# A scan block with its additions moved to GpSimd, and its norm's scale and shift to ScalarE

## The chip, the cores and the metric

The kernel runs on one core of one Trainium2 chip. A core has TensorE (PE), VectorE (DVE), ScalarE (ACT), GpSimd (POOL) and a queue that issues transfers (SyncE, SP). The metric is the device time of one execution in microseconds (us); lower is better. The median of three executions of the kernel before is 11580.11 us (11578.98 to 11580.71).

## The reference

The input is x (8 images, 64 x 64 places, 96 channels). Layer 0 is a two-dimensional selective scan, layer 1 a linear attention and a feed-forward net with simulated 8-bit floats. Cut to what matters here:

```python
xz = group_norm(x) @ in_proj_w.T;  xh, z = split(xz)          # 192 channels each
xc = silu(depthwise_conv3x3(xh) + conv_b)
s0, s1 = xc[..., diag], xc[..., anti]                         # two orders of the 4096 places
xs = stack([s0, s1, reversed(s0), reversed(s1)])              # K = 4 directions
dts, Bs, Cs = split(einsum(xs, x_proj_weight))
delta = softplus(dt_projs(dts) + bias)
h = h * exp(delta * A) + (delta * u) * B                      # scan, 16 states a channel
y = einsum(h, C) + D * u                                      # summed over states, then directions
yn = (y - mean(y)) * rsqrt(var(y) + 1e-5) * ln_w + ln_b       # over the 192 channels
x = x + (yn * silu(z)) @ out_proj_w.T
t = x + attention(ln(x));  out = t + ffn_float8(ln(t))
```

## The kernel before, in words

**The scan loop.** `run` walks 128 steps: 8 images, two passes each (q = 0 forward, q = 1 backward over the time axis; both diagonal orders lie in the two halves of the 128 partitions), 8 chunks of 512 places a pass. A step has 16 iterations, one for each state n; an iteration handles three groups g of 128 partitions x 512 places. One iteration i does the following, spread over neighbouring iterations. ACT makes `decay` for i+2 (L985) and, for most states, `feedT` for i+2 (L1007: `duT` times the state's B; for n = 6 POOL does it, L998; for n = 0, 2, 4, 8, 10 DVE multiplies `du` by a row that PE spreads, L1017 and L1032). PE turns `feedT` into the PSUM banks `feed` (L1015). DVE scans (L1028). POOL keeps the last column as the next step's start value (`keep`, L1042) and multiplies the scanned states by C (`read`, L1047) for i-1. PE adds the turned product of i-4 into the PSUM tile `y` (`reduce`, L1061), of which there is one. `h` has six buffers, `decay` three, `cc` (the rows of C, fetched four iterations ahead, L976) five. Each engine runs its instructions in the order in which this loop writes them.

**The prologue of a step** (L905 on) is woven in as an urgent job: projections of the chunk, softplus on ACT with two loads of activation tables, then `du` (delta times u) on POOL (L947) in iteration 3 of the step before, its twelve turns on PE (L953) and three copies into `duT` on ACT (L955) in the iterations after it. `du` and `duT` have two buffers.

**The end of a step** (`place`, L1080 on) copies `y` to SBUF. After a forward step the copy goes to DRAM (`part`). In a backward step PE has added u times D (L1068), and the forward part, loaded at n = 0 into the same buffer tag `ys` and added by an identity matrix (L1074, three matmuls of 512 columns at n = 8, 9, 10); the result is written to DRAM in image order (`wide`).

**Side work.** `front` (convolution of the next image), `measures` (its group norm) and `tail` (`join`, attention and `layers` of the image before) are generators. `Work` places their pieces in the loop: each piece names its engine and an estimated length, `LAGS` says how many iterations it is put after the piece before it when the engine changes (ACT to DVE or POOL to DVE: one; an explicit lag of 0: the same iteration), and a credit for each engine limits how much is taken in an iteration. Two PSUM banks serve all side work. At the start of each image the loop finishes what is left of the side work (`finish`), and then starts the next image's.

**A join** (four tiles of 128 places, 8 joins an image) loads the two orders' outputs, adds them on PE with an identity matrix (L665), copies the sum to SBUF on ACT (L672) and takes its statistics from PSUM on DVE, in the same iteration (L675). POOL and ACT make the reciprocal root (`rsqrt`), ACT normalizes (L681), PE turns (L687), DVE multiplies by the gate silu(z) (L689), and PE projects. There the norm's scale ln_w is in the weights (`w_ln`, L701), and its shift enters as a second product of the gate with `b_ln` (L704). ACT copies the projection (L708), DVE takes statistics of the same PSUM bank in the same iteration (L713); `layers` does that too (L809, L813). The last image's tail runs after the loop, with more banks; there DVE adds the two orders (L656).

Of the kernel before, what the change touches and what calls it, by code (L numbers as in the profile page):

```python
# [17 lines left out]
P = 128  # L18
# [48 lines left out]
def weights(tc, const, dram, w):  # L67
# [29 lines left out]
    k.w_ln = tile("w_ln", [HC, 2, DM])  # L97
    k.b_ln = tile("b_ln", [HC, 2, DM])
# [93 lines left out]
    def layers():  # L192
# [8 lines left out]
        with tc.tile_pool(name="prep", bufs=1, side="right") as prep:  # L201
            w_out = load("w_out", [HC, 2, DM], w["w_out"], pool=prep)
            ln_w = load("ln_w", [HC, 2], w["ln_w"], pool=prep)
            ln_b = load("ln_b", [HC, 2], w["ln_b"], pool=prep)
            for _ in range(2):
                yield SPIN

            for a in range(2):
                nc.vector.tensor_scalar(k.w_ln[:, a, :], w_out[:, a, :], ln_w[:, a : a + 1], None, ALU.mult)
                nc.vector.tensor_scalar(k.b_ln[:, a, :], w_out[:, a, :], ln_b[:, a : a + 1], None, ALU.mult)  # L210
# [405 lines left out]
def tail(tc, work, x, out, k, at, b, last=False):  # L616
# [4 lines left out]
    with tc.tile_pool(name=f"t1_{b}", bufs=1, **area) as p1:  # L621
# [5 lines left out]
        with tc.tile_pool(name=f"t2_{b}", bufs=8 if last else 2, **area) as p2:  # L627
# [3 lines left out]
            def join(c):  # L631
# [22 lines left out]
                if last:  # L654
                    yield dve(2.5)
                    nc.vector.tensor_tensor(yn, ys[0], ys[1], ALU.add)  # L656
                    for i in range(4):
                        nc.vector.bn_stats(st[:, i, :], yn[:, i, :])
                        nc.vector.bn_aggr(mv[:, i, :], st[:, i, :])
                for j in range(0 if last else 2):  # L660
                    ps = yield bank(0.65)
                    v = view(ps, P, 2, DI)
                    for i in range(2):
                        for d in range(2):
                            nc.tensor.matmul(  # L665
                                v[:, i, :], k.ident, ys[d][:, 2 * j + i, :],
                                start=(d == 0), stop=(d == 1), skip_group_check=True,
                            )
                        if i == 0:
                            yield pe(0.65)  # L670
                    yield act(0.5)
                    nc.scalar.copy(yn[:, 2 * j : 2 * j + 2, :], v)  # L672
                    yield dve(1.0, 0)
                    for i in range(2):
                        nc.vector.bn_stats(st[:, 2 * j + i, :], v[:, i, :])  # L675
                        nc.vector.bn_aggr(mv[:, 2 * j + i, :], st[:, 2 * j + i, :])
                    work.release(ps)
# [5 lines left out]
                for a in range(2):  # L683
# [4 lines left out]
                    yield dve(0.7)  # L688
                    nc.vector.tensor_tensor(yg[:, a, :], v, gate[:, a, :], ALU.mult)  # L689
                    work.release(ps)  # L690
                ps = yield bank(0.65)
# [4 lines left out]
                for i in range(4):  # L696
                    if i % 2 == 0:
                        yield pe(1.2)
                    tok = slice(i * P, (i + 1) * P)
                    for a in range(2):  # L700
                        nc.tensor.matmul(  # L701
                            po[:, i, :], yg[:, a, tok], k.w_ln[:, a, :], start=False, stop=False, skip_group_check=True
                        )
                        nc.tensor.matmul(  # L704
                            po[:, i, :], gate[:, a, tok], k.b_ln[:, a, :], start=False, stop=(a == 1), skip_group_check=True
                        )
# [4 lines left out]
                yield dve(1.7, 0)  # L711
                for i in range(4):
                    nc.vector.bn_stats(st[:, i, :], po[:, i, :])  # L713
                    nc.vector.bn_aggr(mv[:, i, :], st[:, i, :])
                work.release(ps)
# [67 lines left out]
        with tc.tile_pool(name=f"t3_{b}", bufs=8 if last else 3, **area) as p2:  # L783

            def layers(c):
# [25 lines left out]
                yield dve(1.7, 0)  # L811
                for i in range(4):
                    nc.vector.bn_stats(st[:, i, :], po[:, i, :])  # L813
# [478 lines left out]
```

## Time and profile before

| what | value |
|---|---|
| median of 3 | 11580.11 us |
| the profiled execution | 11584.24 us |
| its span | 11582.5 us |
| mean granted TensorE clock | 0.913 |
| PE, DVE, ACT, POOL busy | 9540.5, 9483.5, 9430.0, 8885.1 us |
| L1028 scans on DVE | 6529.7 + 882.5 us |
| L1047 products on POOL | 7076.9 us, 3455 ns each |
| L985 + L1007 on ACT | 3971.1 + 3672.2 us |

The busy time of an engine is a union: two overlapping matmuls count once. The loop runs from 247 us to 11318 us of the span; in its middle an image takes some 1405 us. What comes before is the first image's convolution, what comes after the last image's tail.

### The profile page before, as it was taken

Reading aid. Unit: us, or ns where it says so; the run is one execution under the profiler, and the core shown is the slowest. Engines: PE = TensorE matmul, PEld = TensorE weight load, DVE = VectorE, ACT = ScalarE, POOL = GpSimd, SP = SyncE. Lnnn points to the kernel's source line nnn. Section 1 sums busy time; section 2 is a strip of 40 time slices with the busy share of each in tenths; the row PEclk is TensorE's granted clock in tenths of the full one; section 3 lists DMA queues with packets and bytes.
Section 4 is the critical chain, followed back from the end, with each engine's and each line's share of the span. In section 5 each row is a group of like instructions: output and inputs, shape, how many; then the busy total and the mean of one; then the engine's idle time right before and its main releaser. Section 6 shows DMA issues by size and latency. Waiting matters only on the chain.

```text
span 11582.5 us, 187413 instructions
## 1 busy us (share of the span) xinstructions
PE 9540.5 (82%) x63189; PEld 7973.6 (69%) x63189; DVE 9483.5 (82%) x10714; ACT 9430.0 (81%) x19571; POOL 8885.1 (77%) x6799
## 2 busy tenths in 40 slices
PE   6898889788888888888888888988889888887885
PEld 5677677676776667766677766767667676676663
DVE  2988888888878888788887888888888878888893
ACT  3888888878888888888888788887888878888883
POOL 1877887778867887777887788777887778878883
PEclk8999899898999989999899998999999889898996
DMA  3335333533335333353334433354333533332332
GB/s 91 105 91 140 100 91 91 144 107 97 98 96 134 108 105 91 106 135 104 97 98 113 125 100 104 92 133 116 100 92 98 131 107 96 100 97 86 99 97 53
DMA packets 1122757, 1207.26 MB, mean 104 GB/s; under 512 B 452789, under 2 KB 730006, under 8 KB 1121798
## 3 DMA queue, kind: packets, MB, share of 16 engines
q1 hardware_dynamic: 1121798, 1195.28, 37.6%
q8 instruction: 503, 8.24, 0.3%
q14 instruction: 456, 3.74, 0.1%
HBM read 874.83 MB, written 319.98 MB: 103 GB/s over the span
## 4 chain that ended last, share of the span: by engine, by line
PE 25%; POOL 21%; ACT 20%; DVE 15%; issue 11%; DMA 5%; SPq 3%; POOLq 0%; DVEq 0%; ACTq 0%
POOL h L1047 15%; DVE h L1028 9%; ACT feedT L1007 8%; PE y L1061 7%; PE feed L1015 6%; ACT decay L985 6%; DVE feed L1032 3%; DMA cc<-crow 3%; POOL du L947 2%; PE bank L550 2%; PE bank L915 2%; SPq L595 2%; POOL feedT L998 2%; PE bank L953 1%; POOL carry L1042 1%
## 5 line engine op out<-in xcount | busy, mean ns | idle before, releaser
L1047 POOL TENSOR_TENSOR h<-h,cc 128x1536 f32<-128x1536 f32 x2048 | 7076.9, 3455 | 368.8 <-DMA cc<-crow 187.1
L1028 DVE TENSOR_TENSOR_SCAN h<-decay,carry,feed 128x512 f32<-128x512 f32 x5376 | 6529.7, 1263 | 987.1 <-PE feed L1015 769.8
L985 ACT ACTIVATE decay<-delta,a_neg 128x512 f32<-128x512 f32 x6144 | 3971.1, 712 | 1156.1 <-DVE h L1028 1153.3
L1015 PE MATMUL feed<-ident,feedT 128*128 128x128 f32 x16896 | 3066.7, 301 | 1605.6 <-DVE h L1028 1070.5
L1061 PE MATMUL y<-ident,h 128*128 128x128 f32 x24576 | 3820.9, 288 | 127.2 <-POOL feedT L998 112.8
L1015 PEld LDWEIGHTS feed<-ident,feedT 128*128 128x128 f32 x16896 | 2178.8, 153 | 2288.1 <-ACT feedT L1007 882.8
L1007 ACT ACTIVATE feedT<-duT,rows 128x192 f32<-128x192 f32 x10240 | 3672.2, 444 | 23.8 <-PE feed L1015 21.2
L1061 PEld LDWEIGHTS y<-ident,h 128*128 128x128 f32 x24576 | 3127.9, 150 | 515.5 <-issue 335.2
L1042 POOL COPY carry<-h 128x3 f32<-128x3 f32 x2048 | 393.0, 192 | 1615.3 <-DVE h L1028 1545.8
L1032 DVE TENSOR_TENSOR feed<-feed,du 128x512 f32<-128x512 f32 x1920 | 1202.4, 687 | 137.2 <-PE feed L1017 134.6
L1028 DVE TENSOR_TENSOR_SCAN h<-decay,feed 128x512 f32<-128x512 f32 x768 | 882.5, 1201 | 127.3 <-PE feed L1015 87.5
L550 PE MATMUL bank<-wf,xp 97*128 97x192 f32 x4266 | 858.7, 332 | 0.0
L550 PEld LDWEIGHTS bank<-wf,xp 97*128 97x128 f32 x4266 | 691.0, 194 | 24.1 <-issue 13.5
L1017 PE MATMUL feed<-x,pick 77*128 77x512 f32 x1280 | 695.7, 626 | 3.4
L947 POOL TENSOR_TENSOR du<-delta,u 128x1536 f32<-128x1536 f32 x128 | 441.0, 3445 | 316.1 <-ACT delta L942 309.4
L915 PE MATMUL bank<-wx,u 128*128 128x77 f32 x3048 | 413.1, 299 | 36.2 <-DMA u<-seq 36.2
L915 PEld LDWEIGHTS bank<-wx,u 128*128 128x128 f32 x3048 | 407.3, 217 | 44.4 <-issue 39.6
L937 PE MATMUL bank<-x,ws 13*128 13x512 f32 x764 | 434.7, 649 | 1.6 <-ACT x L928 1.6
L998 POOL TENSOR_TENSOR feedT<-duT,rows 128x512 f32<-128x512 f32 x384 | 396.0, 1061 | 0.0
L955 ACT COPY duT<-bank 128x512 f32<-128x512 f32 x383 | 220.7, 576 | 176.4 <-PE bank L953 174.3
L939 DVE COPY delta<-bank 128x512 f32<-128x512 f32 x382 | 256.2, 671 | 56.4 <-PE bank L937 53.6
L1017 PEld LDWEIGHTS feed<-x,pick 77*128 77x128 f32 x1280 | 209.7, 197 | 71.7 <-DVE h L1028 39.5
(278 smaller groups left out, 7544.3 us busy)
## 6 DMA issues: line engine op xcount, KB each, us to landing
cc<-crow SPq DMA_DIRECT2D x4096, 128.0 KB
u<-seq SPq DMA_DIRECT2D x256, 384.0 KB
wide<-ys SPq DMA_DIRECT2D x512, 192.0 KB
ut<-image SPq DMA_DIRECT2D x768, 64.0 KB
seq<-us SPq DMA_DIRECT2D x128, 384.0 KB
part<-ys SPq DMA_DIRECT2D x64, 768.0 KB
y<-part SPq DMA_DIRECT2D x64, 768.0 KB
y<-wide SPq DMA_DIRECT2D x256, 192.0 KB
```

Of the source, the lines that this page charges most:

```text
L550: nc.tensor.matmul(v[:, j, :], flat[:, o : o + P], k.wf[:, i, :], start=(i == 0), stop=(i == 8), skip_group_check=True)
L915: nc.tensor.matmul(v[:, j, :], u[:, g, j * P : (j + 1) * P], w.wx[:, q, g, :], start=(g == 0), stop=(g == G - 1))
L947: nc.gpsimd.tensor_tensor(du, delta, u, ALU.mult)
L985: nc.scalar.activation(decays[i][:, g, :], made[m].delta[:, g, :], AF.Exp, scale=w.a_neg[:, q, g, n : n + 1])
L998: nc.gpsimd.tensor_tensor(f.rearrange("p (j g) (d c) -> p g j d c", g=G, d=d)[:, g], o.duT.rearrange("p (j g) (d c) -> p g j d c", g=G, d= ...
L1007: nc.scalar.activation(f[part], o.duT[part], AF.Copy, scale=o.rows[:, j, XB + d * NS + n : XB + d * NS + n + 1])
L1015: nc.tensor.transpose(feed[g][:, j * P : (j + 1) * P], feeds[i][:, j * G + g, :], w.ident)
L1017: nc.tensor.matmul(feed[0], w.pick[:, FEED[:n].count("D"), :], made[m].x, start=True, stop=True)
L1028: nc.vector.tensor_tensor_scan(h[:, g, back], a[:, g, back], feed[g][:, back], init, ALU.mult, ALU.add)
L1032: nc.vector.tensor_tensor(feed[g], feed[0], made[m].du[:, g, :], ALU.mult)
L1047: nc.gpsimd.tensor_tensor(hs[i], hs[i], c.unsqueeze(1).to_broadcast([P, G, T]), ALU.mult)
L1061: nc.tensor.matmul(y[:, j, :], hs[i][:, g, r * P : (r + 1) * P], w.ident, is_transpose=True, start=(n == 0 and j % 4 == 0), stop=(n == NS ...
```

## The change

1. The forward part is added to the backward pass's result by POOL, in SBUF, after `y` has been copied (a new urgent job `spread`, two additions of 128 x 768 a backward step); the three identity matmuls go. The part has its own buffer tag `y0` and is loaded at n = 8. In return `du` has one buffer, and its product waits until the step before has used `du` for the last time on DVE (`multiplied`).
2. In a join POOL adds the two orders (except in the last image, where DVE does, as before); PE's additions and ACT's copy go, and DVE takes the statistics from SBUF.
3. ln_w and ln_b are applied by ACT as scale and bias when it copies the turned rows out of PSUM, the gate is multiplied by POOL, and the projection has one product instead of two.
4. The statistics after the projection, and in `layers`, are taken from ACT's copy in SBUF, an iteration after it; the bank is released with the copy.
5. The side work of an image starts at iteration 7 instead of 5 of the image, after the last `spread`.

```diff
-        with tc.tile_pool(name="prep", bufs=1, side="right") as prep:
-            w_out = load("w_out", [HC, 2, DM], w["w_out"], pool=prep)
...
-            for a in range(2):
-                nc.vector.tensor_scalar(k.w_ln[:, a, :], w_out[:, a, :], ln_w[:, a : a + 1], None, ALU.mult)
-                nc.vector.tensor_scalar(k.b_ln[:, a, :], w_out[:, a, :], ln_b[:, a : a + 1], None, ALU.mult)
+        k.w_out = load("w_out", [HC, 2, DM], w["w_out"])
+        k.ln_w = load("ln_w", [HC, 2], w["ln_w"])
+        k.ln_b = load("ln_b", [HC, 2], w["ln_b"])
+        yield SPIN
...
-                for j in range(0 if last else 2):
-                    ps = yield bank(0.65)
...
-                    yield act(0.5)
-                    nc.scalar.copy(yn[:, 2 * j : 2 * j + 2, :], v)
-                    yield dve(1.0, 0)
...
+                else:
+                    yield gp(1.8)
+                    nc.gpsimd.tensor_tensor(yn, ys[0], ys[1], ALU.add)
+                    yield dve(2.1)
+                for i in range(4):
+                    nc.vector.bn_stats(st[:, i, :], yn[:, i, :])
+                    nc.vector.bn_aggr(mv[:, i, :], st[:, i, :])
...
-                    yield dve(0.7)
-                    nc.vector.tensor_tensor(yg[:, a, :], v, gate[:, a, :], ALU.mult)
+                    yield act(0.7)
+                    nc.scalar.activation(
+                        yg[:, a, :], v, AF.Identity, scale=k.ln_w[:, a : a + 1], bias=k.ln_b[:, a : a + 1]
+                    )
                     work.release(ps)
+                yield gp(2.3)
+                nc.gpsimd.tensor_tensor(yg, yg, gate, ALU.mult)
...
-                        nc.tensor.matmul(
-                            po[:, i, :], gate[:, a, tok], k.b_ln[:, a, :], start=False, stop=(a == 1), skip_group_check=True
+                            po[:, i, :], yg[:, a, tok], k.w_out[:, a, :], start=False, stop=(a == 1), skip_group_check=True
                         )
                 yield act(0.5)
                 nc.scalar.copy(t, po)
...
-                yield dve(1.7, 0)
+                work.release(ps)
+                yield dve(1.7)
                 for i in range(4):
-                    nc.vector.bn_stats(st[:, i, :], po[:, i, :])
+                    nc.vector.bn_stats(st[:, i, :], t[:, i, :])
...
         yield gp(3.4)
-        du = o.du = tile("du", [P, G, T])
+        while m and not made[m - 1].multiplied:
+            yield "G", 0.0, -1, False
+        du = o.du = tile("du", [P, G, T], 1)
...
+        if n == FEED.rindex("D"):
+            made[m].multiplied = True
...
-        if q and n in (8, 9, 10) and part == 2:
-            j = n - 8
-            nc.tensor.matmul(
-                y[:, 4 * j : 4 * j + 4, :].rearrange("p a c -> p (a c)"), w.ident,
-                other[m][:, j * T : (j + 1) * T], start=False, stop=False, skip_group_check=True,
-            )
...
-        if q == 0:
-            nc.scalar.copy(ys, y.rearrange("p j c -> p (j c)"))
-            nc.sync.dma_start(out=image(b).part[:, c, :], in_=ys)
-            return
...
+        if q == 0:
+            nc.sync.dma_start(out=image(b).part[:, c, :], in_=ys)
+        else:
+            work.start(spread(m, rows), urgent=True)
+
+    def spread(m, rows):
+        b, q, c = steps[m]
+        for d in range(2):
+            yield gp(1.8, 1)
+            nc.gpsimd.tensor_tensor(
+                rows[:, d], rows[:, d], other[m].rearrange("p (d k c) -> p d k c", d=2, k=TB)[:, d], ALU.add
+            )
...
-            if at == LAG + 1 and b:
+            if at == LAG + 3 and b:
+                work.finish(lambda: all_done() and not other)
                 work.finish(all_done)
                 work.stream(between(b))
```

## The prediction

> **What bounds the kernel now.** I read the page's parts 1, 4 and 5 first, then stretches of the span, then the waits, then the timeline of single steps.
>
> ```profile
> PE 9540.5 (82%) x63189; PEld 7973.6 (69%) x63189; DVE 9483.5 (82%) x10714; ACT 9430.0 (81%) x19571; POOL 8885.1 (77%) x6799
> PE 25%; POOL 21%; ACT 20%; DVE 15%; issue 11%; DMA 5%; SPq 3%; POOLq 0%; DVEq 0%; ACTq 0%
> ```
>
> Four engines are equally full and share the chain: no engine is the bound over the whole span, so time lies in what they wait for. The next view cuts out three stretches of the scan loop: the joins of one image, its layers, and four steps without side work (columns: from:to, length, busy of each engine, TensorE clock, DMA).
>
> ```profile
> 5044.40:5435.60 391.20, 322.46 (x2304) 273.46 (x2304) 320.55 (x420) 307.38 (x670) 303.45 (x303) 0.96 0.39 108
> 5483.20:5757.80 274.60, 222.26 (x1463) 180.82 (x1461) 239.73 (x270) 240.56 (x507) 237.32 (x207) 0.89 0.35 98
> 10883.40:11184.20 300.80, 245.87 (x1640) 201.11 (x1640) 274.22 (x265) 262.52 (x552) 257.19 (x144) 0.92 0.36 100
> ```
>
> Without side work DVE is busy 274.22 of 300.80 (0.912): DVE is the bound, a step (16 iterations) takes 75.2 us. In the joins it is busy 0.82 only; there something stops it. The waits name it:
>
> ```profile
> DVE h L1028 <- PE feed L1015: 857.3, 739, 10.9
> DVE st L713 <- ACT t L708: 135.8, 37, 11.8
> DVE st L675 <- ACT y L672: 109.5, 74, 5.2
> DVE st L813 <- ACT t L809: 71.7, 31, 12.1
> POOL carry L1042 <- DVE h L1028: 1545.8, 755, 13.7
> SPq L976 <- POOL h L1047: 1403.4, 470, 6.2
> ```
>
> Three are same-iteration waits: the statistics follow ACT's copy of the same bank, and that copy stands behind ACT's burst in iteration 3 of each step (softplus, two table loads, a feed, y's copies; 10.15 us). One of them in the timeline (start, length, engine, line):
>
> ```profile
> 5179.76 2.45 DVE L1028 TENSOR_TENSOR_SCAN h<-decay,carry,feed 128x512 f32<-128x512 f32 x2
> 5185.83 0.27 DVE L713 BATCH_NORM_STATS2 st<-bank 128x6 f32<-128x96 f32 x1 [3.61 <-ACT t L708]
> 5182.12 1.47 ACT L1094 COPY ys<-y 128x768 f32<-128x768 f32 x2
> 5183.49 1.95 ACT L985 ACTIVATE decay<-delta,a_neg 128x512 f32<-128x512 f32 x3
> 5185.34 0.46 ACT L708 COPY t<-bank 128x384 f32<-128x384 f32 x1
> ```
>
> POOL, on the other hand, waits 1545.8 us for scans: it has room on average. The rows that price the change:
>
> ```profile
> L947 POOL TENSOR_TENSOR du<-delta,u 128x1536 f32<-128x1536 f32 x128 | 441.0, 3445 | 316.1 <-ACT delta L942 309.4 <-DMA cc<-crow 5.4 <-DMA image<-pre 1.4
> L1074 PE MATMUL y<-y,ident 128*128 128x512 f32 x384 | 196.9, 595 | 0.0
> L704 PE MATMUL bank<-b_ln,gate 96*128 96x96 f32 x928 | 184.7, 282 | 0.0
> L665 PE MATMUL bank<-y,ident 128*128 128x192 f32 x896 | 182.4, 351 | 0.0
> L689 DVE TENSOR_TENSOR yg<-bank,gate 96x512 f32<-96x512 f32 x116 | 78.1, 674 | 17.5 <-PE bank L687 17.2
> L656 DVE TENSOR_TENSOR y<-y,y 128x768 f32<-128x768 f32 x8 | 7.7, 958 | 46.0 <-DMA y<-wide 46.0
> ```
>
> **The change, part by part.** The sum is made against the profiled execution, 11584.2 us (span 11582.5 and 1.7 around it), 4.1 above the median of 11580.1.
>
> POOL gains two-input operations at L947's 3445/1536 = 2.24 ns an element (no row has 768 or 1024 elements; the 384 of L854 take 914 ns, 2.38): 128 additions of 768 for the second pass's parts (1.73 us each, 221), 56 for the joins (97), 64 gates of 1024 (2.31, 148): 466 us, 8885 to 9351. DVE loses 128 gate products of 0.67 (86). PE loses the groups L665, L704 and L1074 (182 + 203 with the last image's + 197). ACT loses 112 copies of 0.47 (L672, 52), gains 128 evacuations at 0.58 to 0.68 (the 512-column copies and biased copies of L604 and L928; 0.63 taken, 81), and y's copy in the 64 first-pass steps becomes two of 0.78 for one of 1.42 (+0.15 each).
>
> *Joins* (seven images). The statistics now follow POOL's addition or ACT's copy an iteration later, so 245.3 us of DVE waits (L713, L675), 35 an image, can go. But POOL rises in the 391.2 us from 303.4 by eight times 1.73 + 2.31 and three steps' additions (3 x 3.46) to 346.1, above DVE's 310: it becomes the fullest. At the 0.912 that the bounding engine reaches without side work that is 379.5: 11.7 saved, 82 in seven images. Bounds: a share of 0.88 saves nothing; all 245 go at best. What PE and DVE lose counts nothing here, since POOL covers it; if POOL kept up, up to 86 of DVE would come on top.
>
> *Layers.* The same move of the statistics (L813, 71.7 us, 9 an image); POOL 237.3 + 10.4 = 247.7, over 0.912 = 271.6, 3 less than 274.6. Between 3 and 9: 6, times seven, 42.
>
> *du with one buffer.* It waits for the previous step's last DVE product, so in the order of the instructions it moves from iteration 3 to 10, its turns (0.6 us of PE each) from the ends of iterations 4 to 6 to those of 11 to 13, ACT's three copies (0.58) from 5 to 7 into 12 to 14. In the bare step, DVE idles 0.30 and 0.68 ahead of iterations 7 and 8 on turns queued behind these; they get 0.30 + 0.44 back. At 12 the copy stands ahead of the feed for iteration 14, where DVE already waits 1.80: 0.58 lost. Where L1074 leaves PE's end of iterations 12 to 14, iteration 0 gets its 0.44 too. Net -0.6 in a second-pass step, -0.16 in a first-pass one: about 15 of the former lie outside the stretches above, all 64 of the latter: -19. Bounds: -77 if all 128 steps gained the 0.6, +74 if the loss alone stays. What is queued behind du at its new place: POOL's later reads, PE's turns of feeds, so DVE.
>
> *y's copies.* The next sums wait for the bank and DVE for a turn behind them at iteration 5: +0.15 x 64 = +10.
>
> *At nothing:* SyncE's issues keep their number; the 4 stores of each half now stand behind POOL's addition, ahead of a fetch that is used four iterations (over 16 us) later and already waits for POOL (1403.4 us); the load of the first pass's part comes 8 iterations later, with 7 left. The convolutions' stretch keeps its work, moved by two iterations. The last image's tail: DVE 10.9 and PE 24 go, POOL 18.5 and ACT 10 come; it is a chain over all engines, 0, bounds -25 to +20.
>
> Sum: 11584 - 82 - 42 - 19 + 10 = 11451; less 4, **11447 us** on the median.
>
> One rule speaks against it. The Trainium skill (GPSIMD Engine Reference, 4.1 Engine selection) gives elementwise work to VectorE, GpSimd being about twice as slow with two inputs; the rows agree (958 against some 1730 ns for 768). Taken as a verdict, all 466 us would count against 317 of waits, 11733; POOL's waits for DVE speak against charging them in full.
>
> **Rivals.**
> *A, slower: du's turns wait for POOL.* Without side work POOL would end du 2.5 us before PE reaches its turn (11084.7 against 11087.2, from the timeline of that step with du's 3.45 put in). In the layers POOL is now 4.6 us behind DVE at that iteration (L1042 starts at 5490.6, the scan ended at 5486.0). With 12 to 14 us more in a join step it falls further behind, and each microsecond past 2.5 stops PE, the feeds and DVE. Some 49 steps are loaded; from 2.7 us in each (133/49) the gain is gone; at 5 it gives 11584 - 133 + 245 - 4 = 11692. Against it: a stall lets POOL catch up, and du no longer waits for softplus.
> *B, nothing gained.* ACT's burst itself holds the feeds, and DVE, freed of one wait, stands in `h <- feed` instead (857.3 us now): 11580. For it: that wait is the largest; against: the statistics' waits come on top of it in the timeline.
> *C, slower: TensorE's clock.* It is at half in places. The joins of images 5 and 6 do the same, with clocks of 0.94 and 0.90, in 288.8 and 293.8 us: 0.04 costs 1.7%. If PE with less work lost 0.04 in all of the loop's 11070 us: +190, 11637. Steps with and without L1074 show the same clock (0.92, 0.91), which speaks against it.
> The Trainium skill (TensorE: Matmul & The Clock Gate, Part 1) says that activity releases the throttle, and that is this rival's reason; the half clock after pauses agrees.
> *D, all waits go:* 11584 - 317 - 4 = 11263; it needs POOL at 0.97 in the joins, which no stretch shows (0.93 in the first step of an image).
>
> **How the numbers follow.** Forecast 0.47 (own range 11360 to 11540), A 0.27, B 0.10, C 0.06, D 0.10. 0.2% is about what the measurement can tell. Faster: 0.47 + 0.10 = 0.57; same: 0.07 of B; slower: A, C and the rest of B, 0.36. The range, 11310 to 11690, leaves out most of D and the upper half of A.
>
> **What would show it.** Right: the statistics' waits on ACT gone, POOL the fullest in the joins at over 0.9, these some 380 us, bare steps within a microsecond of 75. Wrong: PE waiting for du or its turns late in each step (A), the wait for feeds up by 300 (B), a clock under 0.89 (C), joins near 350 (D). DVE waiting for POOL's additions in the joins would be A's mechanism at another place.

## The result and the profile after

The changed kernel takes 11249.32 us (median of 4, 11245.66 to 11260.07), the kernel before 11579.55 beside it: a ratio of 0.972, with a 95% interval of 0.9703 to 0.9737. It is faster by 330 us, where 133 were forecast, and the time lies below the range. The profiled execution has a span of 11243.9 us at a mean clock of 0.907 (0.913 before), so a faster clock is no part of the gain.

The page's part 1 and the engines' line of its part 4, of the kernel after:

```profile
PE 9140.0 (81%) x60885; PEld 7661.4 (68%) x60885; DVE 9396.9 (84%) x10582; ACT 9455.9 (84%) x19651; POOL 9365.4 (83%) x7047
...
PE 24%; ACT 23%; DVE 17%; POOL 14%; issue 10%; DMA 7%; SPq 4%; DVEq 0%; POOLq 0%; ACTq 0%
```

POOL has grown by 480 us and PE has shrunk by 400. POOL's share of the chain nevertheless fell, from 21% to 14%. The stretches of the kernel after (from:to, length, busy of PE, PEld, DVE, ACT, POOL, then clock and DMA): the joins of image 3, its layers, and four steps without side work. They are the same iterations as the three rows of before in the prediction.

```profile
4914.50:5283.40 368.90, 298.24 (x2012) 252.67 (x2013) 313.39 (x417) 311.98 (x673) 344.52 (x336) 0.89 0.43 113
5320.20:5596.60 276.40, 220.13 (x1491) 182.12 (x1491) 249.90 (x291) 245.17 (x521) 251.99 (x219) 0.91 0.40 103
10564.10:10861.40 297.30, 242.75 (x1617) 203.05 (x1617) 273.29 (x265) 262.18 (x553) 270.93 (x153) 0.89 0.38 101
```

The joins went from 391.2 to 368.9 us, with POOL busy 344.5 (0.93), as the fullest. The layers did not gain (274.6 to 276.4). The bare steps went from 75.2 to 74.3 us each. The waits of the kernel after (engine, line, releaser: us in total, times, longest):

```profile
DVE h L1009 <- PE feed L996: 811.6, 729, 4.4
POOL carry L1025 <- DVE h L1009: 803.2, 438, 7.6
DVE st L654 <- POOL y L651: 110.2, 28, 6.5
PEld bank L934 <- POOL du L928: 73.8, 37, 3.9
PE bank L934 <- POOL du L928: 61.8, 35, 3.6
```

The three waits of statistics for ACT (135.8, 109.5 and 71.7 us) are gone from the loop; of the first and the third, 34.5 and 15.8 us are left, all in the last image's tail (24.9 and 12.1 before). One for POOL's additions, 110.2, is new. POOL's wait for scans has halved, from 1545.8 to 803.2. DVE's wait for feeds did not grow. PE's wait for `du`, rival A's mechanism, is there.

Where did the 330 us come from (338.6 between the two profiled executions)? An image's 256 iterations are cut by the starts of POOL's carry copies, and the differences to the kernel before are summed over the eight images (us, worked out from the two traces):

| iterations | what runs beside the loop | after minus before |
|---|---|---|
| 0-16 | border of two images | +23 |
| 16-85 | convolution | -32 |
| 85-125 | walk over the columns (`ut` loads) | -88 |
| 125-192 | joins | -150 |
| 192-200 | end of joins, attention | -71 |
| 200-256 | layers | -4 |
| after the loop | tail of the last image | -18.5 |

These cuts fall inside steps, and `du`'s 3.45 us on POOL stand on the other side of some of them after its move, so the split depends on them. Cut at whole steps (iterations 16, 80, 128, 192, 208 and 256) the same starts give -7, -143, -119, -62 and -13 in place of the five rows from -32 to -4. Either way the joins with their end give 181 to 221 us where 82 were forecast, and 88 to 143 come from a stretch that the prediction put at nothing.

### The profile page after: what moved, and what is told of

It reads as the page before. It is cut to its first block, busy times and chain, and to the rows that moved or that the text cites. A ratio compares the mean times of both kernels' runs of the same rounds, so it can differ in the third digit from the quotient of the medians.

```text
span 11243.9 us, 182845 instructions
## 1 busy us (share of the span) xinstructions
PE 9140.0 (81%) x60885; PEld 7661.4 (68%) x60885; DVE 9396.9 (84%) x10582; ACT 9455.9 (84%) x19651; POOL 9365.4 (83%) x7047
## 4 chain that ended last, share of the span: by engine, by line
PE 24%; ACT 23%; DVE 17%; POOL 14%; issue 10%; DMA 7%; SPq 4%; DVEq 0%; POOLq 0%; ACTq 0%
DVE h L1009 11%; ACT feedT L988 9%; POOL h L1030 8%; ACT decay L966 7%; PE y L1044 7%; PE feed L996 7%; DMA cc<-crow 4%; DVE feed L1013 4%; PE bank L542 3%; SPq L587 2%; PE bank L894 2%; PE feed L998 1%; ACT L63 1%; POOL du L928 1%; DMA y<-wide 1%
## 5 line engine op out<-in xcount | busy, mean ns | idle before, releaser
L996 PEld LDWEIGHTS feed<-ident,feedT 128*128 128x128 f32 x16896 | 2209.1, 155 | 2246.9 <-ACT feedT L988 840.8
L1044 PEld LDWEIGHTS y<-ident,h 128*128 128x128 f32 x24576 | 3164.5, 152 | 525.2 <-issue 410.3
L1025 POOL COPY carry<-h 128x3 f32<-128x3 f32 x2048 | 402.5, 197 | 877.0 <-DVE h L1009 803.2
L894 PE MATMUL bank<-wx,u 128*128 128x77 f32 x3048 | 360.0, 275 | 0.0
L894 PEld LDWEIGHTS bank<-wx,u 128*128 128x128 f32 x3048 | 352.3, 193 | 1.9 <-ACT duT L936 0.2
L934 PE MATMUL bank<-ident,du 128*128 128x128 f32 x1532 | 251.8, 291 | 65.1 <-POOL du L928 61.8
```

What stands on the lines that cost most here:

```text
L894: nc.tensor.matmul(v[:, j, :], u[:, g, j * P : (j + 1) * P], w.wx[:, q, g, :], start=(g == 0), stop=(g == G - 1))
L996: nc.tensor.transpose(feed[g][:, j * P : (j + 1) * P], feeds[i][:, j * G + g, :], w.ident)
L1044: nc.tensor.matmul(y[:, j, :], hs[i][:, g, r * P : (r + 1) * P], w.ident, is_transpose=True, start=(n == 0 and j % 4 == 0), stop=(n == NS ...
```

## The experiments

Ratios are to the kernel before, run beside each, with 95% intervals. "W" is the theory that the gain is DVE's same-iteration waits, "L" that it is the work taken off PE and DVE, "P" that it is the new place of `du`.

**The parts, each alone on the kernel before.** The part named in the change's list is applied, the rest is as before.

`only_stats`: part 4, here after the projection and likewise in the layers.

```diff
-                yield dve(1.7, 0)
+                work.release(ps)
+                yield dve(1.7)
                 for i in range(4):
-                    nc.vector.bn_stats(st[:, i, :], po[:, i, :])
+                    nc.vector.bn_stats(st[:, i, :], t[:, i, :])
...
-                work.release(ps)
```

> The kernel before, with the statistics after the projection and in the layers taken from ACT's copy in SBUF one iteration later, nothing else. Theory W (the gain is the same-iteration waits of DVE on ACT): the waits of L713 and L813 are 207 us, so 80 to 200 us faster. Theory L (the gain is work taken off PE and DVE): nothing is taken off, within 20 us of before. Theory P (the gain is du's new place, which frees the middle of each step): within 20 us of before.

Measured: 11599.44 us, 1.0025 (1.0016 to 1.0035), slower by 29. The waits at the two places did fall, from 207.5 us in sum to 43.4, but DVE's wait for the joins' copies rose from 109.5 to 187.5 and POOL's for `cc` from 187.1 to 295.0. The layers' first loads moved from iteration 194 to 197, and POOL now stops for them at iteration 201 (17.47 us in image 3). So removing waits can be undone by where the lag puts transfers.

`only_du`: `du` with one buffer, its product at iteration 10.

```diff
+        while m and not made[m - 1].multiplied:
+            yield "G", 0.0, -1, False
-        du = o.du = tile("du", [P, G, T])
+        du = o.du = tile("du", [P, G, T], 1)
```

> The kernel before, with du in one buffer and made in iteration 10, nothing else. Theory P: the stretch with the walk of an image (iterations 85 to 119) was 181.5 us before and 168.7 after the whole change, and no other part of the change touches it; image 0, which has no joins or layers, gained 32 us: some 100 us faster in all. Theory W and L: the forecast's -0.16 us in a first-pass step and at best no L1074 to remove in a second-pass one, so within 30 us of before.

Measured: 11561.17 us, 0.9992 (0.9983 to 1.0001). By stretches: -88 in iterations 85-125, -35 in the convolution, -58 in 192-200, but +47 in the joins and +103 in the layers. The -88 is the changed kernel's own: it comes with `du`'s place. In the kernel before, the time from DVE's last scan of iteration 87 to that of iteration 95 is 51.3 us on the mean of the eight images, in this one 38.2, in the changed one 37.4; the eight iterations that follow give 4 back. Most of the -71 of the changed kernel in 192-200 is here too.

`only_join`: part 2, POOL's addition of the two orders, with the statistics an iteration later.

```diff
-                for j in range(0 if last else 2):
-                    ...
-                    yield dve(1.0, 0)
+                else:
+                    yield gp(1.8)
+                    nc.gpsimd.tensor_tensor(yn, ys[0], ys[1], ALU.add)
+                    yield dve(2.1)
```

> The kernel before, with the two orders added by POOL in the joins and their statistics taken from SBUF, nothing else. Theory W: the 109.5 us of waits at L675 go and POOL gets 97 us in the joins, where it has room: 40 to 110 us faster. Theory L: 182 us of PE and 52 us of ACT go, of which little is on the path: 0 to 40 us faster. Theory P: nothing.

Measured: 11491.94 us, 0.9932 (0.9917 to 0.9947), -78.5.

`only_scale`: part 3, scale and shift on ACT, gate on POOL, one projection product.

```diff
-                    yield dve(0.7)
-                    nc.vector.tensor_tensor(yg[:, a, :], v, gate[:, a, :], ALU.mult)
+                    yield act(0.7)
+                    nc.scalar.activation(
+                        yg[:, a, :], v, AF.Identity, scale=k.ln_w[:, a : a + 1], bias=k.ln_b[:, a : a + 1]
+                    )
                     work.release(ps)
+                yield gp(2.3)
+                nc.gpsimd.tensor_tensor(yg, yg, gate, ALU.mult)
...
-                            po[:, i, :], gate[:, a, tok], k.b_ln[:, a, :], start=False, stop=(a == 1), skip_group_check=True
```

> The kernel before, with the norm's scale and shift applied by ACT and the gate by POOL, nothing else. Theory W: no same-iteration wait goes, so within 25 us of before. Theory L: 86 us of DVE and 203 us of PE go and POOL gets 148 us where it has room: 20 to 80 us faster; the last image's tail alone, 18.6 us shorter in the whole change, should show here.

Measured: 11517.17 us, 0.9953 (0.9936 to 0.9969), -53, of which -15.5 in the tail after the loop. That explains most of the changed kernel's -18.5 there.

`only_spread_du`: part 1 and part 5, POOL's addition of the forward part with `du`'s new place.

```diff
-        if q and n in (8, 9, 10) and part == 2:
-            ...
+            work.start(spread(m, rows), urgent=True)
```

> The kernel before, with the first pass's part added by POOL, and with du in one buffer as that needs the room: the whole change without the joins' and layers' parts. Less the run with du's move alone it gives the price of the additions. All theories: 197 us of PE go at a place where ACT sets the pace, 221 us of POOL come where it has room: within 30 us of the run with du's move alone. A POOL that is the bound would make it 50 to 200 us slower than that run.

Measured: 11515.08 us, 0.9958 (0.9941 to 0.9975), -52.5, or -43.5 beyond `du`'s place.

The parts alone sum to 29 - 78.5 - 53 - 52.5 = -155, less than half of 330. They need each other, and the other runs ask how.

**The same-iteration wait.** `lag_psum` is the kernel before with nothing but the lags: the same statistics from the same banks, one iteration after the copy.

```diff
-                yield dve(1.7, 0)
+                yield dve(1.7, 1)
...
-                    yield dve(1.0, 0)
+                    yield dve(1.0, 1)
```

> The kernel before, with all three kinds of statistics still read from PSUM, but one iteration after ACT's copy, the bank held until then. Theory W in its pure form, the wait alone and no work moved: 100 to 280 us of the 317 go. If the banks (two for all side work) bind, holding one longer gives part of it back, and it is less faster than the sum of the runs that take the statistics from SBUF. Theory L or P: within 20 us of before.

Measured: 11401.05 us, 0.9861 (0.9846 to 0.9875), -167. `after_same_iter` does the reverse: the changed kernel with part 4's statistics back in the copy's iteration.

```diff
-                yield dve(1.7)
+                yield dve(1.7, 0)
```

> The kernel after, with the statistics of the projection and of the layers put back into the iteration of ACT's copy (still read from SBUF): the same work on every engine. Theory W: DVE waits for ACT again as at L713 and L813, 207 us before: 80 to 200 us slower than after. Theory L or P: within 20 us of after.

Measured: 11410.84 us, 0.9865 (0.985 to 0.9879), some 168 us above the changed kernel by the ratios. Three numerals give half of the gain, and undoing two of them in the changed kernel costs as much again. So a lag of one iteration is worth about half. Not all of that is the wait, as W has it, for the lag also sets places: in `after_same_iter` the layers' first loads come at iteration 200 instead of 202, and POOL stops behind them at iteration 204, where the changed kernel has no stop:

```profile
5428.88 3.43 POOL L1030 TENSOR_TENSOR h<-h,cc 128x1536 f32<-128x1536 f32 x1 [11.56 <-DMA cc<-crow]
```

Against the changed kernel it loses 98 us in the steps of the joins (iterations 128 to 192) and 71 in the step with that stop (192 to 208). By the two profiles `lag_psum` gains 310 us in the iterations 16 to 256 and gives 117 back in the first 16, at the images' borders.

**POOL as the bound.** `after_gate_twice` lets POOL multiply by the gate twice (its output has an extra factor, so it only serves to price the work).

```diff
+                nc.gpsimd.tensor_tensor(gate, yg, gate, ALU.mult)
                 nc.gpsimd.tensor_tensor(yg, yg, gate, ALU.mult)
```

> The kernel after, with the gate's product in each join done twice by POOL (the output has an extra factor of the normalized rows and the gate): 64 x 2.31 = 148 us more of POOL, 130 of it in the joins under the loop. The forecast's step, POOL is the bound of the joins: 100 to 150 us slower than after. If POOL at 0.93 of the joins still has room and something else sets their time: under 40 us slower.

Measured: 11361.4 us, 0.9824 (0.981 to 0.9839), some 120 us above the changed kernel by the ratios. The joins of image 3:

```profile
4939.50:5324.90 385.40, 303.71 (x2011) 256.85 (x2012) 314.05 (x417) 311.68 (x672) 362.77 (x344) 0.87 0.38 108
```

18.2 us more of POOL made the stretch 16.5 longer. Adding work to POOL costs it nearly in full. Does taking work away pay as well? `after_gate_dve` gives the gate product to DVE, `after_join_dve` the joins' addition.

```diff
-                yield gp(2.3)
-                nc.gpsimd.tensor_tensor(yg, yg, gate, ALU.mult)
+                yield dve(1.1)
+                nc.vector.tensor_tensor(yg, yg, gate, ALU.mult)
```

> The changed kernel with the gate product by DVE (in SBUF) instead of POOL. POOL loses 64 of 2.37 us (152, 133 of it under the loop), DVE gets 64 of some 1.28 (958 ns for 768 elements), 82. POOL is at 0.93 in the joins, DVE at 0.85. If POOL alone bounds the joins: 344.5 - 19 = 325.5 over 0.93 is 350 a join for 368.9, -19 each, about -130 against the changed kernel. If DVE, now with 324 as full as POOL, sets the pace at 0.912: 355, -14 each, -95. If the two already hold each other up so that POOL's room buys nothing: +0 to +84 (10 more of DVE at 0.85).

Measured: 11201.72 us, 0.9688 (0.9673 to 0.9702). This version beats both kernels: 37 us below the changed one by the ratios, less than a third of the 130 that POOL as the only bound would give. Its joins:

```profile
4900.40:5263.10 362.70, 289.68 (x2011) 243.36 (x2012) 327.27 (x425) 311.50 (x672) 332.50 (x328) 0.92 0.41 115
```

```diff
-                    yield gp(1.8)
-                    nc.gpsimd.tensor_tensor(yn, ys[0], ys[1], ALU.add)
+                    yield dve(1.0)
+                    nc.vector.tensor_tensor(yn, ys[0], ys[1], ALU.add)
```

> The changed kernel with the joins' addition by DVE instead of POOL: POOL loses 56 of 1.74 us (97), DVE gets 56 of 0.96 (54). If POOL bounds the joins: -14 us of POOL each over 0.93, -15 a join, about -100 against the changed kernel. If DVE is next at 321 of 355: nearer -90; if DVE and POOL hold each other up: 0 to +60.

Measured: 11284.62 us, 0.9759 (0.9742 to 0.9775), some 45 above the changed kernel. DVE's 56 additions took 110.7 us instead of the 54 expected; the last section tells why.

**What the parts need of each other.** `lag_psum_du` joins the two that touch only order: lags of 1 and `du`'s new place (the edits of `lag_psum` and `only_du`).

```diff
-                yield dve(1.7, 0)
+                yield dve(1.7, 1)
...
+        while m and not made[m - 1].multiplied:
+            yield "G", 0.0, -1, False
```

> The kernel before with two edits: all statistics one iteration after ACT's copy, and du's new place. Alone the first gave -167 us and the second -9. If du's gain in the walk over the columns (-88 over eight images) is real and was only lost again behind the same-iteration waits in the joins and layers (+47 and +103), it stays here: -167 - 88 = -255, some 11313, ratio 0.978. If du's place has a cost of its own in loaded steps (rival A), the two only add: -176, some 11392, 0.985 or above.

Measured: 11472.24 us, 0.9918 (0.9904 to 0.9933), -93: `du`'s place makes this kernel 73 us slower than `lag_psum`. By stretches it gains 369 us in iterations 16 to 256 and loses 254 in the first 16. At the border the loop halts for layers that are not done: iteration 5 of image 3 takes 47 us from last scan to last scan (6.5 before). The joins end later in the planned order with the lag (last Gram sum at iteration 199, before at 183), and later again with `du`'s turns at their new place (211). The layers follow, and 159 of their instructions lie past iteration 256 in `lag_psum`, 286 here, none before. `lag_psum_du_border` moves the border two iterations on, as part 5 does.

```diff
-            if at == LAG + 1 and b:
+            if at == LAG + 3 and b:
```

> The kernel with lagged statistics and du's new place (-93), its images' border (where the planned order halts the loop until the last image's layers are done) moved from iteration 5 to iteration 7, as in the changed kernel. Theory F (the gain of lag and du is given back at the border: there 46.7 us stand in one iteration of each image, +254 us in the first 16 iterations over all images, for layers that reach four iterations past the border): most of it comes back, -93 - 200 or more, under 11280, ratio 0.975 or less. Rival A (du's new place costs in loaded steps): the border's stall only moves, -93, some 11472.

Measured: 11467.92 us, 0.9917 (0.9902 to 0.9931), no gain: the same 286 instructions are left, and iteration 7 takes 36 us in place of iteration 5. That time is given back at the border is seen in the trace; that two more iterations would cure it, as theory F had it, was wrong.

`join_stats` (the edits of `only_join` and `only_stats`) and `join_stats_du` (with `only_du`'s too) are the changed kernel without its scale part and without POOL's addition of the forward part, the first without `du`'s move.

```diff
+                    nc.gpsimd.tensor_tensor(yn, ys[0], ys[1], ALU.add)
...
+                    nc.vector.bn_stats(st[:, i, :], t[:, i, :])
```

> The kernel before with the joins' addition on POOL and all statistics one iteration later from SBUF, du at its old place. The two alone gave -78.5 and +29: -50 if they add, ratio 0.996. If it is the lag alone that counts, -167 as with the banks, 0.986. Against the same with du's new place (-133) it also gives what du's place is worth where nothing waits in the copy's iteration: -83 in the first case, +34 in the second.

Measured: 11408.19 us, 0.9858 (0.9842 to 0.9875), -157.

```diff
+        while m and not made[m - 1].multiplied:
```

> The changed kernel without the scale and gate part and without POOL's addition of the first pass's part: the joins' addition on POOL, all statistics an iteration later from SBUF, du's new place. Alone the two parts left out gave -53 and (with du) -52.5, or -43.5 beyond du. If these two add to the rest as they did alone, this stands at -330 + 53 + 43.5 = -234, some 11335, ratio 0.980. If the gain is nearly all from lag and du, it stands at -255 or more, 0.978 or less; if PE's and DVE's saved work is needed for most of it, at -165, the sum of the single parts, 0.986 or above.

Measured: 11432.15 us, 0.9884 (0.9869 to 0.9898), -133. Here too `du`'s move costs, 24 us, in spite of its gain in the walk. So `du`'s move earns nothing when it is alone (-9) or joined to the lag or to `join_stats`. What it is worth inside the whole change stays open, for no run has the changed kernel with `du` at its old place: the second buffer was given up for `y0`.

`after_no_spread` adds the scale part to that (the edits of `only_scale`; PE adds the forward part as before), `after_no_scale` POOL's addition of the forward part.

```diff
-            work.start(spread(m, rows), urgent=True)
+        if q and n in (8, 9, 10) and part == 2:
+            ...
```

> The changed kernel with the first pass's part added by PE into the bank as before (undoes POOL's addition of the parts, 221 us of POOL, and brings PE's 197 back), border at iteration 5. If the parts' gains add as they did alone: -330 + 43.5 = -287, ratio 0.975. If POOL is the bound, taking 221 us from it makes it faster than the changed kernel, under 0.972. If PE's work is what the rest needs gone, -186 (the kernel without both, -133, and the scale's -53), 0.984.

Measured: 11224.35 us, 0.9705 (0.969 to 0.9719), not to be told from the changed kernel. POOL's 221 us against PE's 197 is an even trade.

```diff
-                    yield act(0.7)
-                    nc.scalar.activation(
-                        yg[:, a, :], v, AF.Identity, scale=k.ln_w[:, a : a + 1], bias=k.ln_b[:, a : a + 1]
-                    )
+                    yield dve(0.7)
+                    nc.vector.tensor_tensor(yg[:, a, :], v, gate[:, a, :], ALU.mult)
...
+                            po[:, i, :], gate[:, a, tok], k.b_ln[:, a, :], start=False, stop=(a == 1), skip_group_check=True
```

> The changed kernel with the norm's scale and shift in the projection's weights and DVE's gate product as before. If the parts add as alone: -330 + 53 = -277, ratio 0.976. If this part with its fewer planned microseconds of PE and DVE (2 of 1.2 down to 0.65, 2 of DVE's 0.7 gone) is what lets the lagged chain keep its time: -133 - 43.5 = -176, ratio 0.985.

Measured: 11427.77 us, 0.9882 (0.9868 to 0.9897), -138. Taking the scale part away costs some 187 us by the ratios, though alone it gave 53. Two things are in it: places in the order, and work. In this kernel the layers' first loads are issued at iterations 197 to 201, and POOL stops for 17.4 us in iteration 201. SyncE's queue and POOL in the timeline (start, length, engine, line):

```profile
5398.48 7.43 SPq L783 DMA_DIRECT2D t<-mid  x1
5405.96 0.67 SPq L781 DMA_DIRECT2D xaT<-turned  x1
5406.67 8.34 SPq L783 DMA_DIRECT2D t<-mid  x1
5415.11 4.69 SPq L1096 DMA_DIRECT2D wide<-ys  x4
5419.84 6.86 SPq L964 DMA_DIRECT2D cc<-crow  x6
```

```profile
5427.63 3.46 POOL L1037 TENSOR_TENSOR h<-h,cc 128x1536 f32<-128x1536 f32 x1 [17.42 <-DMA cc<-crow]
5431.04 3.42 POOL L935 TENSOR_TENSOR du<-delta,u 128x1536 f32<-128x1536 f32 x1
```

The fetch of `cc` stands in SyncE's queue behind two loads of 7.43 and 8.34 us and four stores; POOL waits for it, and `du`, now right behind, reaches PE late (5.27 us of waiting in the trace): rival A's path, set off by a transfer. In the kernel before, the loads come at 194, in the changed one at 202. `no_scale_late2` keeps this kernel's work and puts the joins' end and the layers where the changed kernel has them, by two iterations more between gate and projection.

```diff
-                ps = yield bank(0.65)
+                ps = yield bank(0.65, 2)
```

> The changed kernel without the scale part (which alone of the four parts, taken away, costs nearly all: -138 for -330), but with two iterations more between the gate's product and the projection, which puts the joins' end at iteration 197 and the layers' first steps at 208, 212 and 216, where the changed kernel has them (191, 203, 204 and 220 without). The operations stay those of the kernel without the scale part. Theory O (the part counts by where it puts the joins and the layers' first loads in the planned order): most of it comes back, -280 to -330, ratio 0.976 or less. Theory L (by the 182 us of PE and 86 of DVE that it takes away): only the 20 us stall at iteration 201 goes, seven times some 10 to 15, so -138 - 100 at most, 0.980 or above.

Measured: 11373.08 us, 0.9828 (0.9813 to 0.9843), -198. So some 60 of the 187 us are places in the order (the layers' +53 are gone, and so is the stop), and some 125 are left for work. Which work? Its joins:

```profile
4945.70:5329.10 383.40, 313.91 (x2129) 269.83 (x2129) 320.51 (x431) 299.03 (x652) 326.45 (x328) 0.88 0.38 109
```

`after_gate_dve` has the joins and the layers at the same places. There DVE (327.3 for 320.5), POOL (332.5 for 326.5) and ACT (311.5 for 299.0) are busier; PE alone has less, 24.2 us (289.7), and the stretch is 20.7 shorter. By elimination what counts is PE's work, the second projection product. The granted clock differs too, 0.88 here and 0.92 there: by rival C's two rows (0.04 of clock for 1.7%) some 6.5 of the 20.7 us could be the clock's, an estimate, and these two runs do not separate them.

`gate_dve_no_spread` undoes both POOL additions that had bought little: the edits of `after_gate_dve` and `after_no_spread`.

```diff
-                nc.gpsimd.tensor_tensor(yg, yg, gate, ALU.mult)
+                nc.vector.tensor_tensor(yg, yg, gate, ALU.mult)
...
+        if q and n in (8, 9, 10) and part == 2:
```

> The changed kernel with the two POOL parts that bought nothing undone: the first pass's part is added by PE as before, the gate product is made by DVE in SBUF. Alone, against the changed kernel, -12 for the one and -41 for the other (ratios 0.9705 and 0.9688 to the kernel before, 0.972 for the changed one). If POOL's room counts: -50 together, ratio 0.967 to 0.968. If DVE, then the fullest, takes the place of POOL as the bound: no better than the one alone, 0.969 or above.

Measured: 11253.98 us, 0.9723 (0.9707 to 0.974): worse than `after_gate_dve` by some 40. With POOL relieved, PE's 197 us are no longer an even trade.

## Why the prediction was wrong

**Two steps failed.** Of the 197 us between forecast and result, the first step has to do with the joins, the second with a stretch that was put at nothing.

**The first: "What PE and DVE lose counts nothing here, since POOL covers it".** It made the fullest engine's busy time over 0.912 the length of a join stretch. Put into that sum, the measured share does give the length: 344.5 over 0.934 is 368.9, and 0.912 would have given 378. But the share is no constant of the bounding engine. POOL has 0.94 of the stretch in `after_gate_twice`, 0.92 in `after_gate_dve` and only 0.85 in `no_scale_late2`, which has PE's second product. In the joins POOL's work counts nearly in full (+18.2 gave +16.5), and PE's counts too (-24 gave -20.7, less what the clock may have), at a share of PE of only 0.82. That fits four engines that wait for each other in turn in every iteration; it was not followed instruction by instruction. The scale part's work, PE's second product above all (184.7 us by its row), was worth some 125 once the waits of the statistics were gone. Alone, with its places, the part gave 53. The sum's -82 measured -150 (-119 at whole steps), with the end of the joins -221 (-181).

**The second: "The convolutions' stretch keeps its work, moved by two iterations", at nothing.** In the walk over the columns it gave -88 (-143 at whole steps), the largest item that was not priced. In the kernel before, PE stands there once in each of six images for transfers, with the turns of the feeds queued behind it: for the `ut` that it turns, and for the `u` of the next step's projections. The same instructions of the changed kernel wait for nothing. Image 3 in the timeline, first before, then after (start, length, engine, line):

```profile
4864.00 1.09 PE L602 MATMUL bank<-ident,ut 128*128 128x128 f32 x4 [6.19 <-DMA ut<-image]
4878.96 4.90 PE L915 MATMUL bank<-wx,u 128*128 128x77 f32 x24 [3.93 <-DMA u<-seq]
```

```profile
4747.53 0.60 PE L594 MATMUL bank<-ident,ut 128*128 128x128 f32 x4
4751.79 2.89 PE L894 MATMUL bank<-wx,u 128*128 128x77 f32 x24
```

Summed over the images these waits are 73 us before and none after. They come and go with `du`'s place: every run with `du` at its old place has 64 to 75 us of them in iterations 80 to 128, every run with the new place none. DVE's wait for feeds in iterations 85 to 125 of image 3 shrank with them:

```profile
DVE h L1028 <- PE feed L1015: 30.7, 20, 8.2
```

```profile
DVE h L1009 <- PE feed L996: 16.3, 14, 2.2
```

POOL's own stop there did not go: it waits 16.47 us for `cc` behind the loads of `ut` before, and 16.02 after, one iteration later (the profile puts this one down to PE, but its scans had long been done, and `cc` is issued only behind a long run of `ut` loads). Why the new place of `du` puts PE's two groups behind their loads was not tested.

**The statistics' waits.** That they can go was right; with the places that the lag moves they are half of the gain, seen in both directions (-167 and +168). Of the 317 us, 37 lay in the last image's tail and stayed. The prediction let them go only as far as POOL's busy time allowed. Rival D priced all of them, and its 11263 is near the time, but its condition did not come (POOL at 0.93, not 0.97): its number is near by luck.

**Layers, -42: wrong.** The stretch took 1.8 us more. The statistics' wait went, but the layers' first loads moved from iteration 194 to 202, and some 30 of their instructions lie past iteration 256, in the next image's first iterations (+23).

**`du`'s move, -19.** The bare steps did as told, -0.87 us for a forecast -0.6. Not priced, besides the walk, was what the move costs elsewhere. Rival A's wait is there (PE 61.8 us, PEld 73.8 over mostly the same time), and the move cost 73 and 24 us in the two pairs of runs, but most of that stands at other places. In the first pair it is the border (254 us given back, 117 without the move), though PE waits only 54.2 us for `du`. In the second, the steps of the joins lose 129 us to the move and PE waits 24.6.

**The tail, 0 with bounds of -25 to +20:** -18.5, inside the bounds, nearly all from the scale part. **At nothing, SyncE's queue:** in the changed kernel that held, but only by where the loads fall. In `only_stats`, `join_stats_du` and `after_no_scale` they begin at iteration 197, five earlier than in the changed kernel, and from carry copy to carry copy POOL then takes 21, 26 and 24 us at iteration 201 of image 3 (7.1 in the changed kernel). **y's copies, +10,** were not measured by themselves. **Rivals B and C:** DVE's wait for feeds did not rise (857.3 to 811.6), and the clock fell by 0.006.

The rule of the Trainium skill that was weighed there (GPSIMD Engine Reference, 4.1 Engine selection), taken as a verdict, would have given 11733. POOL's 480 us more did not decide it, and in small it went both ways: giving the gate product back to DVE was worth 37 us, giving DVE the joins' addition cost 45.

What stays open: why the parts' sum falls short in each pair, and above all why `du`'s move, which gains in the walk in every run that has it, is paid for in the joins or at the border in the runs without the scale part. The lag and the places of loads are shown to count, PE's work by elimination; that the longer chains of side work in the planned order are what runs over the border is seen in the iteration numbers, and was not cured by an experiment.

## What to carry to other kernels

In this loop, in which four engines are over 0.8 busy and pass each iteration on to each other, no one engine covered the others. In one like it, price work taken from any of them on the chain, and look for same-iteration waits first: one iteration of slack, with the places that it moved, was worth half of this change. Do not put a stretch at nothing because its work stays: look at its waits. An order written by a planner moves as a whole: after each change, see at which iterations the bursts of transfers fall, and what is queued behind them. Try parts together as well as alone: here the single parts summed to less than half of the whole.

## What the hardware showed that was not expected

An operation of DVE with both inputs in SBUF stands still until POOL's running two-input operation is over. DVE's addition of 768 elements in `after_join_dve` takes 0.94 to 0.96 us when nothing holds it, and up to 3.90 us beside POOL. One of DVE's, and POOL's instructions at that time:

```profile
4995.16 3.87 DVE L651 TENSOR_TENSOR y<-y,y 128x768 f32<-128x768 f32 x1
```

```profile
4994.76 3.45 POOL L928 TENSOR_TENSOR du<-delta,u 128x1536 f32<-128x1536 f32 x1
```

POOL's `du` ends at 4998.21, and DVE's addition 0.82 us later: DVE counts as busy, but seems to work only from there. All 30 of the 56 that took over 1.1 us began while such an operation of POOL was running, and all 30 ended 0.81 to 0.82 us after it did. In `after_gate_dve` the gate product took 1.20 us when free and 1.79 on the mean. The Trainium skill (SBUF — State Buffer, "SBUF: two separate sides") says that the two engines share a port pair, which one instruction holds to its end, and that a DVE operation with two SBUF inputs is held up by it; the trace agrees. DVE's products of a feed in PSUM with `du` (687 ns before, 685 after, with POOL 480 us fuller) show none of it.

Single loads also took long in SyncE's queue: 7.43 and 8.34 us for one `t` each, where six fetches of `cc` took 6.86 in the same lines.
